# A graph network layer on one core: the last tile of every tenth gather group, fetched row by row through SyncE

## The chip, the cores and the metric

The kernel runs on one core of one Trainium2 chip. The metric is the device time of one execution in microseconds (us). Lower is better. The names of the engines are those of the profile: PE is the matrix engine (PEld its weight loads), DVE the vector engine, ACT the scalar engine, POOL GpSimd and SP SyncE. A name with a q, such as SPq, is that engine's sequencer, the part that waits, loads registers and issues DMAs.

## The reference

One message-passing layer over a graph with 12,500 nodes and 412,500 edges, the edges sorted by receiver:

```python
h = jnp.maximum(_layernorm(x, axis=-1), 0.0)
msg_in = jnp.concatenate([h[src], h[dst], edge_attr_32], axis=-1)       # 64 + 64 + 32
messages = swish(msg_in @ W1 + b1) @ W2 + b2
att = softmax(swish(msg_in @ Wa1 + ba1) @ Wa2 + ba2, axis=0)            # over all edges
aggregated = segment_sum(messages * att, dst, num_segments=12500)
upd_in = jnp.concatenate([h, aggregated], axis=-1)
out = x + swish(upd_in @ Wu1 + bu1) @ Wu2 + bu2
```

## The kernel before

**Tables.** Because `msg_in @ W` splits into a sender's, a receiver's and an edge's part, the kernel first computes two tables in device memory, one row of 128 floats (512 B) for each node: `ts_d` for the sender's part and `tr_d` for the receiver's part, each with the attention branch in columns 0 to 63 and the message branch in 64 to 127. They are written by lines 237 (SP) and 252 (ACT).

**Groups.** The edges are then worked off in one pass (`one_pass`), in groups of K = 8 tiles of P = 128 edges. There are T = 3224 tiles and NG = 403 groups. For each group g:

- `load(g)`, lines 366 to 401. POOL issues eight gathers (line 373). Each is one indirect DMA that fetches, for 128 edges, the row of `ts_d` that the edge's `src` names, into one of the eight slices of `gs`, a tile of 128 x 8 x 128 floats. The pool `gather` (line 170) holds eight such tiles. SP fetches the edges' features (`eo`, line 382) and receivers (`db`, line 385) for NQ = 4 groups at a time, and for every group two windows of `tr_d` rows into `wins` (line 392), whose place comes from a register; three `wins` buffers take turns. The registers are loaded four at a time (`registers`, line 360, a TENSOR_LOAD). DVE builds the one-hot matrix (line 396), and PE forms the receivers' and edges' part in PSUM (`pe`, line 400).
- `begin(g)`, lines 403 to 406. DVE adds `pe` and `gs` into `gs` (line 405); ACT takes the tanh (line 406).
- `end(g)`, lines 408 to 431. DVE forms messages and attention logits (lines 416 to 427).
- `by_node`, `out_of`, `project` and `put`, some five groups later. DVE weighs one-hot windows (line 468), PE sums the messages by node (lines 474 and 485), DVE adds them into `sums` (lines 495 to 499).

**Order.** The loop of lines 535 to 585 runs `begin(g)`, `load(g + 2)` and `end(g)` in turn, so PE's part of a group stands two groups ahead of the addition that needs it. Most DVE, PE and ACT instructions are pinned to program order; DMAs are not, and a scheduler places them. Each engine works its own queue in order. In the built program SP's DMAs carry eight semaphores in turn, and each DMA waits until the DMA that last used its semaphore, eight places back in the queue, has landed; POOL's gathers have eight of their own. SP's `wins` DMA for group g also waits until PE has read the same buffer for group g - 3.

**Beside it and behind it.** From group 16 on, once every four groups until the 98 blocks of nodes are done, `node_rest` and `node_bias` send five or six more DMAs through SP (lines 270, 279, 288, 290). Behind the pass, lines 588 to 630 compute the nodes' output. `general` is another path, taken only when the receivers spread too far; it is not taken here.

Of the kernel before, what the change touches and what calls it, by code (L numbers as in the profile page):

```python
# [42 lines left out]
F32 = mybir.dt.float32  # L43
I32 = mybir.dt.int32
AF = mybir.ActivationFunctionType
ALU = mybir.AluOpType
AX = mybir.AxisListType
ENG = mybir.EngineType
# [3 lines left out]
P = 128  # L52
# [3 lines left out]
C = 2 * U  # L56
S1 = U + 1
K = 8
# [7 lines left out]
B = 4  # L66
NQ = 4
TABLES = 4
EPS = 1e-5
NEG = -3.0e38  # L70
BIG = 3.0e38
WHY = "a receiver's number; windows past the last node are padded"


@with_exitstack
def gnn_kernel(ctx: ExitStack, tc: tile.TileContext, n_edges, x, src, dst, dst_row, first, edge,
               W1, b1, W2, b2, Wa1, ba1, Wa2, ba2, Wu1, bu1, Wu2, bu2, out):
    nc = tc.nc
    NB = x.shape[0] // P
    T = src.shape[1]  # L80
    NG = T // K
    NP = NB * P
# [6 lines left out]
    ts_d = dram.tile([NP, C], F32, name="ts_d")  # L89
# [13 lines left out]
    for r in range(2):  # L103
        for h, eng in ((0, nc.sync), (1, nc.scalar)):
            rows = slice(h * D, (h + 1) * D)
# [67 lines left out]
    with tc.tile_pool(name="node1", bufs=1) as node1, \  # L173
# [31 lines left out]
        for c in range(0, NB, CB):  # L205
# [9 lines left out]
            nc.vector.tensor_reduce(rstd, sq, AX.X, ALU.add)  # L215
            nc.vector.tensor_scalar(rstd, rstd, 1.0 / D, EPS, op0=ALU.mult, op1=ALU.add)
            nc.scalar.activation(rstd, rstd, AF.Sqrt)
# [5 lines left out]
            for b in range(0, CB, 8):  # L223
                n = min(8, CB - b)
# [16 lines left out]
        for c in range(0, NB, CB):  # L241
            tr = node.tile([P, CB, C], F32, name="tr")
            for b in range(0, CB, 4):
                n = min(4, CB - b)
                pn = node_ps.tile([P, 4, C], F32, name="pn", bufs=3)
                for i in range(0, n, 2):
# [5 lines left out]
            nc.scalar.dma_start(tr_d[:NP, :].rearrange("(p b) f -> p b f", b=NB)[:, c:c + CB, :], tr)  # L252

    one_pass(tc, n_edges, locals())
    again = nc.values_load(wrong[0:1, 0:1], min_val=0, max_val=1,
                           skip_runtime_bounds_check_because="it is the outcome of a comparison")
# [36 lines left out]
def one_pass(tc, n_edges, v):  # L293
    nc = tc.nc
    NB, T, NG, NP, CB = (v[k] for k in ("NB", "T", "NG", "NP", "CB"))
# [3 lines left out]
    ts_d, tr_d, bq_d, edge, dst_row = (v[k] for k in ("ts_d", "tr_d", "bq_d", "edge", "dst_row"))  # L299
# [8 lines left out]
    pin = tc.keep_in_program_order  # L308

    with ExitStack() as ctx:  # L310
# [22 lines left out]
        for w in wins:  # L333
            nc.vector.memset(w, 0.0)
            for r in range(2):
                rows = slice(WR + r * DE, WR + (r + 1) * DE)
                nc.vector.tensor_copy(w[rows, :, r, :], we[rows, None, :].to_broadcast([DE, 2, C]))
        with tc.tile_pool(name="work2", bufs=2) as work2, \
                tc.tile_pool(name="small", bufs=3) as small, \
                tc.tile_pool(name="pre_ps", bufs=AHEAD + 1, space=PSUM) as pre_ps, \  # L340
                tc.tile_pool(name="one_ps", bufs=1, space=PSUM) as one_ps:
            pes, gss, lgs, ps_, psums, sps, pps, ees, mts = ({} for _ in range(9))


            w2t_ps = one_ps.tile([P, 4, P], F32, name="mt")[:U, 0, :S1]
# [4 lines left out]
            nc.tensor.matmul(w2u_ps, w2t, wu1a, start=True, stop=True)  # L350
            nc.vector.tensor_copy(w2u, w2u_ps)
            at_sp, at_dve = {}, {}


            tr_w = bass.AP(tensor=tr_d.tensor, offset=tr_d.offset,
# [2 lines left out]
            def registers(g, engine, at):  # L358
                n = min(NQ, NG - g)
                _, regs = nc.values_load_multi_w_load_instructions(  # L360
                    base_sb[0:1, g:g + n], engines=[engine], min_val=0, max_val=NP - 1,
                    skip_runtime_bounds_check_because=WHY)
                for i in range(n):
                    at[g + i] = regs[i]

            def load(g):

                t = g * K
                if g % NQ == 0:
                    registers(g, ENG.SP, at_sp)  # L370
                gs = gss[g] = gather.tile([P, K, C], F32, name="gs")
                for j in range(K):
                    nc.gpsimd.indirect_dma_start(  # L373
                        out=gs[:, j, :], out_offset=None, in_=ts_d[:, :],
                        in_offset=bass.IndirectOffsetOnAxis(ap=src_sb[:, t + j:t + j + 1], axis=0))
                if g % NQ == 0:
                    n = min(NQ, NG - g) * E2
                    eo = work2.tile([P, NQ, E2], F32, name="eo")
                    db = work2.tile([WR, NQ, E2], I32, name="db")
                    for i in range(g, min(g + NQ, NG)):  # L380
                        ees[i] = eo[:, i - g, :], db[:, i - g, :]
                    nc.sync.dma_start(eo.rearrange("p g e -> p (g e)")[WR:, :n],
                                      edge[:, g * E2:g * E2 + n])
                    for r in range(2):
                        nc.sync.dma_start(
                            db.rearrange("p g e -> p (g e)")[r * R:(r + 1) * R, :n],
                            bass.AP(tensor=dst_row.tensor, offset=dst_row[r:r + 1, g * E2:].offset,
                                    ap=[[0, R], [1, n]]))
                eo, db = ees.pop(g)
                win = wins[g % WINS]  # L390
                for r in range(2):
                    nc.sync.dma_start(win[r * R:(r + 1) * R, :, r, :],
                                      tr_w[bass.ds(at_sp[g], R), :, :])
                for h in range(2):
                    e = slice(h * E2 // 2, (h + 1) * E2 // 2)
                    pin(nc.vector.tensor_scalar(eo[:WR, e], db[:, e], bj[:, g, h:h + 1], None,  # L396
                                                op0=ALU.is_equal))
                pe = pes[g] = pre_ps.tile([P, K, C], F32, name="pe")
                for q in range(H):
                    pin(nc.tensor.matmul(pe[:, 2 * q:2 * q + 2, :], eo[:, q * P:(q + 1) * P],  # L400
                                         win[:, q // 2, :, :], start=True, stop=True))

            def begin(g):

                pin(nc.vector.tensor_tensor(gss[g], pes[g], gss[g], ALU.add))  # L405
                pin(nc.scalar.activation(pes[g], gss[g], AF.Tanh))  # L406

            def end(g):
# [123 lines left out]
            for g in range(AHEAD):  # L532
                load(g)
            done = 0
            for g in range(NG):
# [3 lines left out]
                if more and g == NG - 1:  # L539
                    next(more)  # L540
                begin(g)
                if more and g < NG - 1:
                    next(more)
# [6 lines left out]
                if g + AHEAD < NG:  # L550
                    load(g + AHEAD)
# [36 lines left out]
        with tc.tile_pool(name="upd1", bufs=1) as upd1, \  # L588
# [14 lines left out]
            for c in range(0, NB, 2 * H):  # L603
                n = min(H, (NB - c) // 2)
# [32 lines left out]
def general(tc, n_edges, v, dst):  # L637
# [7 lines left out]
    with ExitStack() as ctx:  # L645
        keep = ctx.enter_context(tc.tile_pool(name="keep_g", bufs=1))
        act_d = dram.tile([P, T, S1], F32, name="act_d")
        sum_d = [dram.tile([NP + P, S1], F32, name=f"sum_d{r}") for r in range(TABLES)]
        before = keep.tile([P, P], F32, name="before")
# [15 lines left out]
        rows = (NP + P) // P  # L665
        for r in range(TABLES):
            flat = sum_d[r].rearrange("(p b) f -> p (b f)", p=P)
# [63 lines left out]
        with tc.tile_pool(name="sums_g", bufs=2) as work, \  # L731
                tc.tile_pool(name="sums_g_ps", bufs=2, space=PSUM) as sums_ps:
            for g in range(0, T, G):
# [3 lines left out]
                for k in range(0, ng, K):  # L737
# [26 lines left out]
                    for j in range(K):  # L764
                        nc.gpsimd.indirect_dma_start(
                            out=sum_d[(t + j) % TABLES][:, :],
                            out_offset=bass.IndirectOffsetOnAxis(ap=to[:, j:j + 1], axis=0),
# [6 lines left out]
        with tc.tile_pool(name="upd_g", bufs=2) as work, \  # L774
                tc.tile_pool(name="upd_g_ps", bufs=2, space=PSUM) as upd_ps:
            for c in range(0, NB, CB):
                part = work.tile([P, TABLES, CB, S1], F32, name="part")
                for r in range(TABLES):
                    nc.sync.dma_start(part[:, r], sum_v[r][:, c:c + CB, :])
                for r in range(1, TABLES):  # L780
                    nc.vector.tensor_tensor(part[:, 0], part[:, 0], part[:, r], ALU.add)
# [71 lines left out]
```

## Time and profile before

| | |
|---|---|
| median of 3 runs | 4180.05 us (4179.7 to 4185.37) |
| the profiled execution's own time | 4179.44 us |
| its span, first to last instruction | 4177.7 us |
| mean granted clock of PE | 0.635 of full speed |
| first and last gather (line 373) start | 75.3 and 4103.8 us |
| busy: POOL, DVE, PE, ACT | 3048.7, 2879.0, 2250.2, 600.1 us |

The span is counted from the first instruction of the profiled execution to its last; its own time is 1.7 us more. "Busy" is the time in which an engine worked, so POOL is busy for 73% of the span. An engine's wait, and the register and DMA-issuing instructions of a sequencer, are not counted as busy; they are found in the views by line and in the timeline. In the lists by group a line reads: source line, engine, operation, output and inputs, count, then busy time, mean time of one, and the idle time before it with what ended it.

### The profile page before, as it was taken

To read this page: it belongs to the slowest core of one execution; us is meant where nothing else is said; L and a number is where in the kernel's file an instruction comes from. 1 tells how busy PE (TensorE), PEld (TensorE's weight loads), DVE (VectorE), ACT (ScalarE), POOL (GpSimd) and SP (SyncE) were. 2 spreads that over 40 slices of the span, in tenths; PEclk is the share of its full clock that TensorE was granted. 3 is DMA by queue.
4 is the path that set the end of the run, shared out by engine and by line. 5 is a ranking of instruction groups with operands and counts; after the bars stand their busy time and mean duration, and the time that the engine had idled before them with its cause. 6 is when DMAs were issued, how large, how long until landed. Compare 5 with 4: busy or idle time off the path is not lost.

```text
span 4177.7 us, 43813 instructions
## 1 busy us (share of the span) xinstructions
PE 2250.2 (54%) x10980; PEld 1686.0 (40%) x10980; DVE 2879.0 (69%) x7713; ACT 600.1 (14%) x1229; POOL 3048.7 (73%) x3236
## 2 busy tenths in 40 slices
PE   5644556445555555555555555555555555555555
PEld 4433344333334433444334443343444334434344
DVE  5766767666767766766666666676676666766668
ACT  3211111111111111111111111111111111111112
POOL 2777777777777777777777777777777777777772
PEclk9566666666666666656666566566565665666665
DMA  6433334333333333333333333333323333333323
GB/s 246 112 86 101 101 95 102 96 100 103 95 95 91 83 88 89 81 89 83 87 89 80 89 86 84 90 80 90 90 80 90 82 88 90 80 90 82 87 77 110
DMA packets 232283, 392.22 MB, mean 94 GB/s; under 512 B 99797, under 2 KB 158294, under 8 KB 218838
## 3 DMA queue, kind: packets, MB, share of 16 engines
q0 software_dynamic: 103168, 211.49, 19.0%
q1 hardware_dynamic: 125808, 167.82, 15.3%
q10 hardware_dynamic: 3046, 10.02, 0.6%
q8 instruction: 91, 1.49, 0.2%
q14 instruction: 170, 1.39, 0.1%
HBM read 363.29 MB, written 25.72 MB: 93 GB/s over the span
## 4 chain that ended last, share of the span: by engine, by line


## 5 line engine op out<-in xcount | busy, mean ns | idle before, releaser
L373 POOL DMA_INDIRECT gs<-ts_d,src_sb x3224 | 3047.1, 945 | 1055.2 <-issue 884.1
L400 PE MATMUL pe<-wins,eo 128*128 128x256 f32 x3224 | 1405.3, 612 | 1183.2 <-issue 1132.6
L400 PEld LDWEIGHTS pe<-wins,eo 128*128 128x128 f32 x3224 | 959.6, 312 | 1460.3 <-issue 1198.1
L405 DVE TENSOR_TENSOR gs<-pe,gs 128x1024 f32<-128x1024 f32 x403 | 492.0, 1221 | 1115.7 <-DMA gs<-ts_d,src_sb 1108.2
L406 ACT ACTIVATE pe<-gs 128x1024 f32<-128x1024 f32 x403 | 415.6, 1031 | 2777.4 <-DVE gs L405 2315.9
L468 DVE TENSOR_SCALAR wt<-iota_w,dloc,p 128x40 f32<-128x40 f32 x3224 | 726.1, 317 | 0.1
L474 PE MATMUL sp<-wt,acts 128*65 128x40 f32 x6448 | 586.0, 261 | 0.9 <-DVE wt L468 0.9
L474 PEld LDWEIGHTS sp<-wt,acts 128*65 128x65 f32 x6448 | 535.3, 173 | 27.0 <-DVE wt L468 1.0
L444 PE MATMUL mt<-ident,mx 128*128 128x128 f32 x103 | 48.4, 470 | 515.0 <-DVE sums L498 508.8
L416 DVE SCALAR_TENSOR_TENSOR acts<-pe,gs 128x512 f32<-128x512 f32 x403 | 272.0, 675 | 27.6 <-ACT pe L406 27.6
L424 DVE TENSOR_TENSOR pe<-pe,wa 128x512 f32<-128x512 f32 x403 | 281.6, 699 | 12.8
L422 DVE SCALAR_TENSOR_TENSOR pe<-pe,gs 128x512 f32<-128x512 f32 x403 | 280.6, 696 | 11.5 <-ACT pe L406 0.2
L427 DVE TENSOR_REDUCE lg<-pe 128x8 f32<-128x512 f32 x403 | 276.9, 687 | 10.4
L396 DVE TENSOR_SCALAR eo<-db,bj 64x256 f32<-64x256 int32 x806 | 274.1, 378 | 7.6
L485 PEld LDWEIGHTS mt<-ss,w2u 65*64 65x64 f32 x806 | 99.8, 175 | 396.4 <-issue 383.4
L485 PE MATMUL mt<-ss,w2u 65*64 65x40 f32 x806 | 150.8, 281 | 162.9 <-DVE gm L451 150.9
L444 PEld LDWEIGHTS mt<-ident,mx 128*128 128x128 f32 x103 | 18.6, 180 | 528.2 <-DVE sums L498 521.1
L455 ACT ACTIVATE scale<-fall 128x1 f32<-128x1 f32 x103 | 20.9, 203 | 514.2 <-DVE fall L454 514.2
L499 DVE COPY sums<-nmax 64x40 f32 x403 | 79.6, 198 | 9.1 <-issue 0.3
L480 ACT COPY ss<-sp 65x40 f32<-65x40 f32 x403 | 73.4, 182 | 25.5 <-PE sp L474 25.3
L498 DVE TENSOR_TENSOR sums<-sums,mt 64x40 f32 x300 | 53.5, 178 | 2.9 <-PE mt L485 1.6
L275 ACT COPY bu<-mt 64x512 f32<-64x512 f32 x24 | 25.8, 1076 | 150.1 <-PE mt L272 144.4
(96 smaller groups left out, 596.7 us busy)
## 6 DMA issues: line engine op xcount, KB each, us to landing
gs<-ts_d,src_sb POOLq DMA_INDIRECT x3224
eo<-in_edge_dram SPq DMA_DIRECT2D x100, 512.0 KB
db<-in_dst_row_dram SPq DMA_DIRECT2D x200, 256.0 KB
wins<-tr_d SPq DMA_DIRECT2D x806, 32.0 KB
ts_d<-ts SPq DMA_DIRECT2D x7, 896.0 KB
tr_d<-tr ACTq DMA_DIRECT2D x7, 896.0 KB
xc<-in_x_dram SPq DMA_DIRECT2D x7, 448.0 KB
hT_d<-hT ACTq DMA_DIRECT2D x1, 3136.0 KB
```

Source lines behind the costliest of these rows:

```text
L373: nc.gpsimd.indirect_dma_start(out=gs[:, j, :], out_offset=None, in_=ts_d[:, :], in_offset=bass.IndirectOffsetOnAxis(ap=src_sb[:, t + j:t ...
L396: pin(nc.vector.tensor_scalar(eo[:WR, e], db[:, e], bj[:, g, h:h + 1], None, op0=ALU.is_equal))
L400: pin(nc.tensor.matmul(pe[:, 2 * q:2 * q + 2, :], eo[:, q * P:(q + 1) * P], win[:, q // 2, :, :], start=True, stop=True))
L405: pin(nc.vector.tensor_tensor(gss[g], pes[g], gss[g], ALU.add))
L406: pin(nc.scalar.activation(pes[g], gss[g], AF.Tanh))
L416: pin(nc.vector.scalar_tensor_tensor(acts[g % ACTS][:, :, 0:U], th[:, :, U:C], 1.0, gs[:, :, U:C], op0=ALU.add, op1=ALU.mult))
L422: pin(nc.vector.scalar_tensor_tensor(att, th[:, :, 0:U], 1.0, gs[:, :, 0:U], op0=ALU.add, op1=ALU.mult))
L424: pin(nc.vector.tensor_tensor(att, att, wa2[:, None, :].to_broadcast([P, K, U]), ALU.mult))
L427: pin(nc.vector.tensor_reduce(lgs[s][:, k:k + K], att, AX.X, ALU.add))
L468: pin(nc.vector.tensor_scalar(wt[:, j, :], iota_w[:, j // H, :], dloc[:, g * K + j:g * K + j + 1], p[:, k + j:k + j + 1], op0=ALU.is_equal ...
L474: pin(nc.tensor.matmul(sp, acts[g % ACTS][:, j, :], wt[:, j, :], start=j == 0, stop=j == K - 1))
L485: pin(nc.tensor.matmul(pp, w2u, sps.pop(g), start=True, stop=True))
```

## The change

For groups 10, 20, ..., 390 (39 of them) the eighth gather is left out. The 128 rows that it fetched come instead into a tile of their own, `one_gs`, over the ten groups before: in each `load(g)`, behind the `wins` DMAs, SP loads 13 of the 128 row numbers from `one_src` into registers with one TENSOR_LOAD (11 in the last of the ten groups) and issues one DMA of 512 B for each. The row numbers come into SBUF with one DMA of 512 B from a new input, `src_row`, the same numbers laid out in one row. In `begin(g)` of such a group the addition of 128 x 1024 becomes one of 128 x 896 and one of 128 x 128, the second reading `one_gs`. `work2` holds two buffers of `one_gs`.

```diff
+EVERY = 10
+ROWS = 13
+LOADS = 13
...
-            pes, gss, lgs, ps_, psums, sps, pps, ees, mts = ({} for _ in range(9))
+            pes, gss, lgs, ps_, psums, sps, pps, ees, mts, alone = ({} for _ in range(10))
...
+            rows_at, rows_to = {}, {}
+
+            def rows(g):
+                if g % EVERY == 0:
+                    t = (g + EVERY) * K + K - 1
+                    rows_to.clear()
+                    if g + EVERY < NG - 4:
+                        rows_to[g + EVERY] = one = work2.tile([P, C], F32, name="one_gs")
+                        alone[g + EVERY] = one
+                        rows_at[0] = small.tile([1, P], I32, name="one_src", bufs=2)
+                        nc.sync.dma_start(rows_at[0], v["src_row"][:, t * P:(t + 1) * P])
+                for to in rows_to.values():
+                    i = g % EVERY * ROWS
+                    for a in range(i, min(i + ROWS, P), LOADS):
+                        n = min(LOADS, P - a)
+                        _, regs = nc.values_load_multi_w_load_instructions(
+                            rows_at[0][0:1, a:a + n], engines=[ENG.SP], min_val=0, max_val=NP - 1,
+                            skip_runtime_bounds_check_because=WHY)
+                        for k in range(n):
+                            nc.sync.dma_start(to[a + k:a + k + 1, :], ts_d[bass.ds(regs[k], 1), :])
...
-                for j in range(K):
+                for j in range(K - (g in alone)):
                     nc.gpsimd.indirect_dma_start(
...
                     nc.sync.dma_start(win[r * R:(r + 1) * R, :, r, :],
                                       tr_w[bass.ds(at_sp[g], R), :, :])
+                rows(g)
...
-                pin(nc.vector.tensor_tensor(gss[g], pes[g], gss[g], ALU.add))
+                n = K - (g in alone)
+                pin(nc.vector.tensor_tensor(gss[g][:, :n, :], pes[g][:, :n, :], gss[g][:, :n, :], ALU.add))
+                if n < K:
+                    pin(nc.vector.tensor_tensor(gss[g][:, n, :], pes[g][:, n, :], alone.pop(g), ALU.add))
...
+        "src_row": padded(src, t * P)[None],
```

More of the change, by code (lines that the diff above doesn't have):

```diff
@@ L75, in gnn_kernel @@
 @with_exitstack
-def gnn_kernel(ctx: ExitStack, tc: tile.TileContext, n_edges, x, src, dst, dst_row, first, edge,
+def gnn_kernel(ctx: ExitStack, tc: tile.TileContext, n_edges, x, src, src_row, dst, dst_row, first, edge,
                W1, b1, W2, b2, Wa1, ba1, Wa2, ba2, Wu1, bu1, Wu2, bu2, out):
```

## The prediction

> **What bounds the kernel now.** I read the page first (busy times and groups), then POOL's timeline at the start, the view of the gathers' line, the waits, and last SP's own queue, since that is where the new work goes.
>
> ```profile
> L373 POOL DMA_INDIRECT gs<-ts_d,src_sb x3224 | 3047.1, 945 | 1055.2 <-issue 884.1
> L405 DVE TENSOR_TENSOR gs<-pe,gs 128x1024 f32<-128x1024 f32 x403 | 492.0, 1221 | 1115.7 <-DMA gs<-ts_d,src_sb 1108.2
> ```
>
> ```profile
> 75.35 1.10 POOL L373 DMA_INDIRECT gs<-ts_d,src_sb  x1 [72.95 <-DMA tr_d<-tr]
> 76.76 0.94 POOL L373 DMA_INDIRECT gs<-ts_d,src_sb  x1 [0.30 <-issue]
> 78.00 0.95 POOL L373 DMA_INDIRECT gs<-ts_d,src_sb  x1 [0.30 <-issue]
> ```
>
> ```profile
> L373 POOL DMA_INDIRECT gs<-ts_d,src_sb x3224: 940/944/1193, 75.3 to 4103.8; - x190
> ```
>
> POOL looks only 73% busy, but 0.30 us stands ahead of nearly every gather and nothing is waited for in it ("issue"): it belongs to the gather. From the first start (75.35) to the end of the last (4103.8 + 0.94) are 4029.4 us; over 3224 gathers that is **1.250 us each**, without a hole. Of the rest, 75 us lie before the first gather and 73 us behind the last. DVE, the next busiest, waits 1108.2 us for gathered rows, 2.75 us per group, so it has room. POOL's queue of gathers sets the end.
>
> SP's queue holds the rest of the evidence:
>
> ```profile
> SPq L392 <- PE pe L400: 1931.4, 275, 22.6
> ```
>
> ```profile
> PE pe L400 <- DMA wins<-tr_d: 14.9, 1, 14.9
> ```
>
> ```profile
> L392 SPq FUSED_REGOPS  x806: 37/37/51, 99.5 to 4062.5; - x162
> L392 SPq MOVE wins<-tr_d x806: 29/29/128, 99.6 to 4062.7; - x162
> L392 SPq DMA_DIRECT2D wins<-tr_d x806: 316/317/790, 99.7 to 4062.7; - x162
> ```
>
> ```profile
> 2022.76 0.82 SPq L392 DMA_DIRECT2D wins<-tr_d  x2
> ```
>
> SP waits 1931 us for PE to free `wins`, while PE waited for `wins` once only: SP runs up to three groups ahead, about 30 us.
>
> **What goes.** 39 gathers (groups 10 to 390) leave POOL's queue: 39 x 1.250 = **-48.7 us**. What is late next? DVE gets such a group after 8.75 us instead of 10.0; 10.0 less its 2.75 us of waiting is 7.25 us of work, so it still waits. Over ten groups POOL takes 79 x 1.250 = 98.7 us, **9.87 us per group**.
>
> **What DVE gains as work.** In 39 groups one addition becomes two. A 64x40 addition takes 0.18 us in the trace, which I take as the price of one more instruction. It also waits on up to eight semaphores of SP's DMAs; a sequencer's semaphore wait is a row of 17 ns with gaps of some 45 ns, so up to 0.5 us. Together 0.7 us, in 2.75 us of waiting: nothing at the end. Without that cover it would be 39 x 0.7 = 27 us.
>
> **What SP gains.** This decides. Two `wins` DMAs take 0.82 us from the first one's start to the second one's end, so start to start is 0.82 - 0.317 = 0.503 us: the DMA's own 0.317 and 0.186 for FUSED_REGOPS, MOVE and gaps. A row's DMA, from a register too, has the same sequence. Its own issue is unknown for one row; the nearest rows are three one-row DMAs of ACT's queue in the prologue:
>
> ```profile
> L137 ACTq DMA_DIRECT2D w2b<-in_b_dram x1: 251/251/251, 16.3 to 16.3; - x1
> L121 ACTq DMA_DIRECT2D base_sb<-in_first_dram x1: 291/291/291, 7.9 to 7.9; - x1
> L110 ACTq DMA_DIRECT2D w_bu<-in_bu_dram x1: 681/681/681, 1.4 to 1.4; - x1
> ```
>
> The bounds are 0.251 and 0.681. I take 0.29: that one stood close behind another DMA, as the rows will; 0.681 is from the program's first two microseconds, where most DMAs took 0.4 to 0.7. A row then costs 0.476 us of SP (0.437 to 0.867), and 12.8 rows per group 6.1 us (5.6 to 11.1).
>
> The TENSOR_LOAD of 13 registers:
>
> ```profile
> L360 SPq TENSOR_LOAD <-base_sb x101: 293/298/676, 98.9 to 4035.1; - x101
> L255 SPq TENSOR_LOAD <-wrong x1: 279/279/279, 4172.1 to 4172.1; - x1
> ```
>
> Four registers take 298 ns and one takes 279, so 6 ns each: 13 take 0.35, with a gap 0.40 us per group. The lower bound is 0.3; the upper one is 13/4 x 0.298 = 0.97, if each register cost in proportion.
>
> Here the Trainium skill speaks against the change. "Runtime: NRT & Kernel Launch", section Instruction fetch mechanics, says that a load into sequencer registers takes about 200 ns for each register, even in bulk. By it, 13 registers would be 2.6 us per group, SP would need 2.2 us more than in the sum below and pass POOL's pace, and by the working of rival 1 the kernel would end some 350 us or more behind the forecast. It speaks of loads from device memory; `base_sb` lies in SBUF, and its 6 ns per register decide.
>
> Per ten groups SP also issues `one_src` and waits for it. `hb<-in_x_dram`, issued at 115.80, released DVE's line 289 at 118.16, 2.0 us after its issue ended, so 2.5 us, 0.25 per group.
>
> Landing: each DMA waits for the one eight places back. Eight rows of 0.476 are 3.8 us, more than those 2.0, so rows alone do not stall. Behind `eo` and two `db` (1 MB, at the best slice's 246 GB/s 4.2 us) a row can wait 4.2 + 2.0 - 3.8 = 2.4 us, once in four groups: up to 0.6 per group.
>
> SP's old work per group: two `wins` 1.0, a quarter of `eo` (0.48), two `db` (0.41) and a TENSOR_LOAD (0.30) with gaps 0.45, semaphore waits 0.1: 1.6 us. While the node work runs (about groups 18 to 116), a quarter of lines 288, 290, 279 and two of 270 (0.40, 0.39, 0.49, 2 x 0.61, gaps) adds 0.7.
>
> The sum per group: 1.6 + 6.1 + 0.4 + 0.25 + (0 to 0.6) = **8.35 to 8.95 us**, and 9.05 to 9.65 with node work, against POOL's 9.87. SP keeps up, narrowly. The `wins` of a group may come up to 30 us late before PE asks for them, and POOL has eight `gs` buffers, so a short excess is absorbed.
>
> Who waits behind a waiting row? The next group's `wins`, then PE's line 400, then DVE's line 405. SP's last rows for group 10m stand behind `wins` of 10m - 1, which PE uses in iteration 10m - 3; the addition that needs them is three groups (30 us) later. The packets carry the same bytes as before; landings shift a little, but POOL waits for none that matters (53 us in 0.3 us pieces, all of them the usual gap).
>
> **Sum.** 4179.4 - 48.7 = 4130.7 for the profiled execution; it lies 0.6 us under the median, so about **4131 us** (-1.2%).
>
> **Rivals.**
> 1. *SP becomes the bound: slower.* In SP's queue, rows hold up `wins`, and PE starves. Load 389, the last with rows, must be done when iteration 388 begins, 75 + 389 x 9.87 + 3 = 3918 us by POOL's pace; SP reaches it at 97 + 390 W + 70 (node work). So it decides from W = 9.62 us, that is a row of (9.62 - 2.85)/12.8 = 0.53 us (0.58 without the stall behind `eo`), and the gain is used up at W = 9.74. Against it: `wins` itself, with 64 rows, takes 0.503. For it: with `db`'s median of 0.414 a row takes 0.60, W is 10.5, and the end comes at 4131 + 97 + 4095 + 70 - 3918 = 4475 us; with 0.681, W is 13.35 and the end 5590.
> 2. *SP falls behind in the node stage only.* At the dearer end (0.503 per row) W is 2.3 + 6.4 + 0.4 + 0.25 + 0.6 = 10.0 there, 0.1 over for 100 groups; with SP's waits for DVE's line 289 and ACT's line 275 (108 and 17 us in the waits) perhaps 60 us of lag, of which 30 of lead and some buffers are cover. Price up to 40 us: 4131 to 4171.
> 3. *The removed gather is not the one that counts:* DVE waits for the last row in each such group for what POOL saves, 1.25 us: 4180. Against it stand the three groups between them.
>
> **How the numbers follow.** The forecast 4131 has 0.72 (4127 to 4136; no more than 39 gathers can be gained), rival 2 has 0.09, rival 3 has 0.04, rival 1 has 0.15. The range, 4126 to 4172, leaves out rivals 1 and 3. A measurement here tells 0.2% (8 us) from no change. Faster: 0.72 + 0.09 = 0.81; within 0.2%: 0.04; slower: 0.15.
>
> **What would show it.** Right: 3185 gathers still 1.25 us apart; line 405 still released by the gathers' DMA; SP's DMA of a row near 0.29 us and start to start near 0.48; a TENSOR_LOAD of 13 near 0.35; SPq still waiting for PE at `wins`, perhaps a third of 1931 us. Wrong: POOL with idle time before gathers released by DVE; PE's line 400 released by `wins` often; rows over 0.53 us apart.

## The result and the profile after

The change made the kernel slower: 4213.40 us (4213.05 to 4216.91, 4 runs) against 4181.07 us (4179.7 to 4185.37, 4 runs), a ratio of 1.0079 with a 95% interval of 1.0065 to 1.0094. The profiled execution took 4216.91 us, with a span of 4215.1 us, 37.4 us more than before. In experiments 1 to 4 the profiled execution of each kernel run more than once was 1 to 8 us shorter than its others, so each ratio is to runs of the kernel before that were taken beside it, and profiled times are compared with profiled times.

In the changed kernel the gathers are line 397, the one-hot 421, PE's receiver part 425, the addition 431 (and 433 for `one_gs`), the row numbers 372, the rows 376, `wins` 416. The groups and the row of the gathers' line:

```profile
L397 POOL DMA_INDIRECT gs<-ts_d,src_sb x3185 | 3019.4, 948 | 1121.1 <-issue 949.9
L425 PE MATMUL pe<-wins,eo 128*128 128x256 f32 x3224 | 1436.9, 623 | 1639.9 <-DMA wins<-tr_d 633.4
L421 DVE TENSOR_SCALAR eo<-db,bj 64x256 f32<-64x256 int32 x806 | 260.5, 361 | 862.0 <-DMA db<-in_dst_row_dram 821.4
L431 DVE TENSOR_TENSOR gs<-pe,gs 128x1024 f32<-128x1024 f32 (+1 forms) x403 | 485.8, 1206 | 80.6 <-PE pe L425 28.5
```

```profile
L397 POOL DMA_INDIRECT gs<-ts_d,src_sb x3185: 938/944/1194, 75.4 to 4141.9; - x200
L397 POOLq EVENT_SEMAPHORE  x398: 42/43/13137, 74.3 to 4125.6; - x199
```

The 39 gathers are gone, yet the last one starts 38.1 us later (4141.9 against 4103.8). DVE's addition hardly waits for gathered rows any more (1108.2 us before, 27.0 now); DVE and PE wait at the start of a group instead, for `db` (821 us) and `wins` (633 us), both of which come through SP. PE's many waits for `wins` are one of the signs that the prediction named as "wrong"; rows over 0.53 us apart, another, did not come. SP's own waits, in its queue, say the same from the other side:

```profile
SPq L372 <- DMA one_src<-in_src_row_dram: 86.1, 37, 4.8
...
SPq L416 <- PE pe L425: 43.9, 15, 9.1
...
SPq L376 <- DMA db<-in_dst_row_dram: 28.6, 36, 1.3
```

The wait for PE at `wins`, SP's spare time, fell from 1931.4 us to 43.9. SP hardly waits for anything: it is always working, and late. Its rows and the gaps of up to 0.2 us between them, taken together, fill some 95% of the time (before, 22% in the node stage and 15% behind it).

Where POOL loses time is seen in its timeline, about 600 us into the run (start, duration, instruction, idle time before it):

```profile
609.79 0.94 POOL L397 DMA_INDIRECT gs<-ts_d,src_sb  x1 [0.31 <-issue]
611.81 0.61 DVE L421 TENSOR_SCALAR eo<-db,bj 64x256 f32<-64x256 int32 x2 [7.16 <-DMA db<-in_dst_row_dram]
...
612.66 3.75 PE L425 MATMUL pe<-wins,eo 128*128 128x256 f32 x8 [7.18 <-DMA one_gs<-ts_d]
...
614.74 0.70 DVE L450 SCALAR_TENSOR_TENSOR pe<-pe,gs 128x512 f32<-128x512 f32 x1
615.47 0.70 DVE L452 TENSOR_TENSOR pe<-pe,wa 128x512 f32<-128x512 f32 x1
616.19 0.94 POOL L397 DMA_INDIRECT gs<-ts_d,src_sb  x1 [5.46 <-issue]
```

POOL stands still for 5.46 us and goes on after DVE's line 450, the last reader of an old `gs`, has ended. The view calls the gap "issue", which reads as if POOL waited for nothing. It waited for a buffer, in its sequencer: that is the EVENT_SEMAPHORE row above, whose longest took 13.1 us. The one before this gap ended at 615.47, 0.04 us after line 450, and so, within 0.05 us, did every one of the 92 that took over 0.5 us. (PE's line 425 does not read `one_gs`, which the view names there; it reads the one-hot that DVE's line 421 finished at 612.42, 0.24 us before.)

By stages (time, then busy time and count of PE, PEld, DVE, ACT and POOL, clock, DMA share, GB/s), before and then after:

```profile
600.00:1450.00 850.00, 457.33 (x2294) 333.30 (x2295) 597.34 (x1630) 124.65 (x254) 642.76 (x681) 0.65 0.37 95
1450.00:4000.00 2550.00, 1373.36 (x6698) 1032.59 (x6697) 1745.20 (x4722) 324.43 (x702) 1928.14 (x2041) 0.62 0.33 86
```

```profile
600.00:1450.00 850.00, 459.80 (x2104) 331.76 (x2102) 550.86 (x1503) 117.31 (x233) 586.51 (x619) 0.61 0.36 91
1450.00:4000.00 2550.00, 1392.64 (x6857) 1052.81 (x6858) 1788.71 (x4863) 339.20 (x721) 1928.18 (x2034) 0.63 0.35 87
```

All the loss lies in the node stage: there POOL did 619 instructions in place of 681. Behind it POOL runs at its old rate (2034 against 2041), with fewer gathers to a group, so the other engines get through more groups.

The account of POOL's queue closes. 39 x 1.250 = -48.7 us. Of the gaps between gathers 25 were longer than 0.5 us (the 22 over 1.3 us all lie between 600 and 1480 us); above the usual 0.305 they add +77.1. A gather took 948.0 ns on average and not 945.1: 3185 x 2.9 ns = +9.1. The sum is +37.5; the last gather came 38.1 us later and the span grew by 37.4.

DVE's steps show SP's pace. Line 431 started for group 40 at 533 us, for group 120 at 1404, for 140 at 1600 and for 380 at 3943: **10.9 us per group** in the node stage and **9.76** behind it, against POOL's 9.87. When DVE began group 20 POOL was 4.1 groups ahead of it, at group 60 it was 6.9, with eight buffers in all (2.2 at both places before): the buffers were used up by 600 us, and from there SP's excess of 1 us per group came straight out of POOL's time.

And one instruction makes SP's excess, as experiments 1 and 5 will show. The rows of the new work, and SP's timeline in two stretches of the later stage:

```profile
L372 SPq TENSOR_LOAD <-one_src x390: 970/2832/3262, 101.0 to 4017.0; - x195
```

```profile
L376 SPq FUSED_REGOPS  x4992: 37/37/47, 102.0 to 4023.7; - x200
L376 SPq MOVE one_gs<-ts_d x4992: 29/29/42, 102.1 to 4023.8; - x200
L376 SPq DMA_DIRECT2D one_gs<-ts_d x4992: 224/228/308, 102.2 to 4023.8; - x200
```

```profile
2004.44 0.86 SPq L416 DMA_DIRECT2D wins<-tr_d  x2
2008.40 5.24 SPq L376 DMA_DIRECT2D one_gs<-ts_d  x13
```

A row's DMA costs less than was forecast: 0.228 us of its own, and 13 of them take 5.24 us, so (5.24 - 0.228)/12 = 0.42 us from start to start (0.476 forecast). But from the end of `wins` (2005.30) to the first row (2008.40) stand 3.1 us, and 2.86 of them are the TENSOR_LOAD of 13 numbers. On average it took 2.28 us, not 0.35. Even the old load of four numbers, 298 ns before, had grown:

```profile
L384 SPq TENSOR_LOAD <-base_sb x101: 313/496/682, 99.0 to 4072.4; - x101
```

The 390 loads are not alike. They go by where in `one_src` the 13 numbers begin:

| first number | begins at a multiple of | TENSOR_LOAD, us (usual values) |
|---|---|---|
| 0, 52, 104 | 4 words | 0.97 to 1.18 |
| 26, 78 | 2 words, not 4 | 2.68 or 2.86 |
| 13, 39, 65, 91 | 1 word | 2.86 |
| 117 (11 numbers) | 1 word | 2.46 |

### The profile page after: what moved, and what is told of

Its sections match the earlier page's. It is cut to its first block, busy times and chain, and to the rows that moved or that the text cites. A ratio compares the mean times of both kernels' runs of the same rounds, so it can differ in the third digit from the quotient of the medians.

```text
span 4215.1 us, 59401 instructions
## 1 busy us (share of the span) xinstructions
PE 2284.3 (54%) x10980; PEld 1713.3 (41%) x10980; DVE 2885.7 (68%) x7752; ACT 609.6 (14%) x1229; POOL 3020.9 (72%) x3197
## 4 chain that ended last, share of the span: by engine, by line
## 5 line engine op out<-in xcount | busy, mean ns | idle before, releaser
L425 PE MATMUL pe<-wins,eo 128*128 128x256 f32 x3224 | 1436.9, 623 | 1639.9 <-DMA wins<-tr_d 633.4
L425 PEld LDWEIGHTS pe<-wins,eo 128*128 128x128 f32 x3224 | 980.5, 319 | 1928.1 <-issue 1666.5
L421 DVE TENSOR_SCALAR eo<-db,bj 64x256 f32<-64x256 int32 x806 | 260.5, 361 | 862.0 <-DMA db<-in_dst_row_dram 821.4
L431 DVE TENSOR_TENSOR gs<-pe,gs 128x1024 f32<-128x1024 f32 (+1 forms) x403 | 485.8, 1206 | 80.6 <-PE pe L425 28.5
```

The costliest lines, as they stand in the source:

```text
L431: pin(nc.vector.tensor_tensor(gss[g][:, :n, :], pes[g][:, :n, :], gss[g][:, :n, :], ALU.add))
```

## The experiments

Two theories were open. **A**: SP became the bound by its own work, through the load of the registers, whose price hangs on the place of the first number. **B**: SP is held by the landings of the small DMAs, each of which waits for the one eight places back. A third possibility was that the work itself is hidden and the rows disturb the gathers in memory.

**1. `e1_aligned`: the same numbers, each group's 13 beginning at a multiple of 16 words.**

```diff
-rows_at[0] = small.tile([1, P], I32, name="one_src", bufs=2)
+rows_at[0] = small.tile([1, EVERY * 16], I32, name="one_src", bufs=2)
...
-rows_at[0][0:1, a:a + n]
+rows_at[0][0:1, i // ROWS * 16:i // ROWS * 16 + n]
...
-"src_row": padded(src, t * P)[None],
+"src_row": ...   # (t, 10, 16): 13 numbers, then 3 zeros
```

> The same rows, with the row numbers laid out so that each group's 13 begin on a multiple of 16 words; nothing else changes. Theory A (SP is the bound, by the load of 13 registers, which is slow where its first word is not on a multiple of four): the load falls from 2.29 us on average to 1.0 to 1.2 us in every group, SP needs 9.7 us per group in the node stage and 8.6 behind it against POOL's 9.87, POOL never stalls, and the time is 4131 us (4127 to 4140). Theory B (SP's queue is held up by landings, each DMA waiting for the one eight places back, or PE and DVE by later windows and receivers behind the rows): the load may shorten, but the queue waits instead, and the time stays over 4180 us.

Measured: 4142.89 us (4141.34 to 4143.33) against 4185.79 for the kernel before, measured beside it, a ratio of **0.9897** (0.9881 to 0.9914): the same rows, the same number of DMAs (`one_src` alone grows from 512 to 640 B), and the loss is a gain. The time lies 3 us over the range expected; the kernel before was itself some 5 us slower beside it (4185.79 against 4181.07). The load, POOL's line and the stages:

```profile
L372 SPq TENSOR_LOAD <-one_src x390: 971/1157/1655, 101.0 to 3903.8; - x195
```

```profile
L397 POOL DMA_INDIRECT gs<-ts_d,src_sb x3185: 940/947/1194, 75.6 to 4066.6; - x200
L397 POOLq EVENT_SEMAPHORE  x398: 42/43/43, 74.5 to 4050.3; - x199
```

```profile
600.00:1450.00 850.00, 476.98 (x2292) 349.59 (x2291) 598.25 (x1624) 124.44 (x251) 643.02 (x678) 0.64 0.42 98
1450.00:4000.00 2550.00, 1419.28 (x6820) 1065.32 (x6818) 1781.93 (x4825) 329.76 (x713) 1929.56 (x2035) 0.62 0.37 88
```

POOL's semaphore waits are all 43 ns, no gap is over 0.5 us, and the node stage has 678 POOL instructions again. DVE does fall behind there, to 4.9 groups at group 120 (10.15 us per group), and catches up later (1.2 at group 160): the eight buffers cover it. The line of additions shows who is late again:

```profile
L431 DVE TENSOR_TENSOR gs<-pe,gs 128x1024 f32<-128x1024 f32 (+1 forms) x403 | 487.4, 1210 | 750.2 <-DMA gs<-ts_d,src_sb 715.9
```

This version is faster than both kernels. B falls: as many small DMAs land as in the change, and by B the time would have stayed over 4180 us.

**2. `e2_no_rows`: the gathers go, and nothing comes in their place.** The eighth tile of the 39 groups lacks the sender's part.

```diff
+                if g % EVERY == 0 and 0 < g < NG - 4:
+                    alone[g] = None
...
-                rows(g)
...
-nc.vector.tensor_tensor(gss[g][:, n, :], pes[g][:, n, :], alone.pop(g), ALU.add)
+nc.vector.tensor_copy(gss[g][:, n, :], pes[g][:, n, :])
```

> The gather of the eighth tile is left out in the same 39 groups and nothing is fetched in its place, so the sender's part of those 39 tiles is left out; DVE still does two instructions there. Both theories: POOL saves 39 x 1.250 us and nothing takes its place, 4131 us (4129 to 4134). A third reading, that a gather less does not shorten POOL's queue by its whole slot, would give 4140 to 4180.

Measured: 4137.16 us (4130.27 to 4137.76), a ratio of 0.9884 (0.9867 to 0.99). The profiled execution took 4130.27 us, 48.2 less than before's beside it (4178.51). Its median is 2 us over the range expected.

```profile
L399 POOL DMA_INDIRECT gs<-ts_d,src_sb x3185 | 3010.4, 945 | 1043.2 <-issue 882.7
```

So the term of the removed gathers was right to 0.5 us, and it is all that leaving them out can gain. Experiment 1 is 5.7 us above it by the medians, 11.1 by the profiled executions. In the latter the gathers account for it: 948.4 ns in place of 945.2, times 3185, is 10.4 us. The rows are not shown to be the reason: in experiment 3, with as many rows in each of its 270 groups, a gather took 945.4 ns on average, and in experiment 4, with one row per group, 947.9.

**3. `e3_from_130`: rows for groups 130 to 390 only, so none while the node work runs.** The loads stay where they were, seven of ten at a dear place.

```diff
-                    if g + EVERY < NG - 4:
+                    if 120 <= g and g + EVERY < NG - 4:
...
+                        if g == 120:
+                            pin(nc.vector.memset(rows_at[0], 0))
```

> Rows only for groups 130, 140, ..., 390 (27 of them), fetched from load 120 on, behind the node stage; the loads of registers are as in the changed kernel. Theory A, with the stage where SP falls behind being the node stage: behind it SP needs 9.78 us per group against POOL's 9.87, POOL never stalls, 27 x 1.250 = 33.7 us are saved: 4147 us (4143 to 4153). The reading that the rows cost as much wherever they stand: 27/39 of the 32 us lost, some 4204 us.

Measured: 4154.33 us (4147.3 to 4154.94), a ratio of 0.9925 (0.9908 to 0.9941); profiled 4147.3 us. 27 gathers x 1.25 = 33.8 us under 4178.5 would be 4144.8. The median is 1 us over the range expected, and far from the 4204 of the other reading.

```profile
L374 SPq TENSOR_LOAD <-one_src x270: 972/2851/2878, 1276.7 to 3923.3; - x135
```

```profile
SPq L418 <- PE pe L427: 497.5, 95, 22.4
```

The loads are as dear as in the change (2.28 us on average), and POOL has no gap over 0.5 us: behind the node stage SP's pace fits within POOL's 9.87, with little to spare, and the whole loss is made in the node stage. (Part of SP's wait for PE is from the groups before the first rows.) The old load of four numbers shows a second effect here: 0.31 us in the groups before the first rows and 0.50 from there on, always from a multiple of four.

**4. `e4_probe`: the price of the load by itself.** The kernel before, with one more TENSOR_LOAD in each group, of 1, 2, 4, 8, 13 or 16 words, from 16 different places of `base_sb`, and one row's DMA (into a tile that DVE clears first).

```diff
+n, a = (1, 2, 4, 8, 13, 16)[g % 6], 64 + g // 6 % 16
+_, regs = nc.values_load_multi_w_load_instructions(base_sb[0:1, a:a + n], engines=[ENG.SP], ...)
...
+nc.sync.dma_start(dummy, ts_d[bass.ds(regs[n - 1], 1), :])
```

> The kernel before, with one more load of registers per group on SP, of 1, 2, 4, 8, 13 or 16 words from base_sb, its first word at each of 16 places in turn; the last of the registers is used for one row's DMA into a tile that nobody reads. No gather is left out. SP is idle three quarters of the time here. Theory A: 0.28 us for one word and 0.2 us for each further word where the first word is off a multiple of four (13 words 2.7 to 2.9 us, 16 words 3.3 to 3.5), and 0.2 us for each further four words on it (4 words 0.30, 8 words 0.5, 16 words 0.9 to 1.1, 13 words 1.0 to 1.2). Its rival: the load is long in the changed kernel since it waits for what stands ahead of it in a full queue; here all are 0.28 to 0.40 us. The time stays within 0.3% of before under both, since 3.9 us more per group find SP idle.

Measured: 4188.83 us, one run. All its loads, and by size and place:

```profile
L395 SPq TENSOR_LOAD <-base_sb x403: 274/977/4123, 100.4 to 4088.7; - x135
```

| words | first at a multiple of 4 | at 2 words past | at an odd word |
|---|---|---|---|
| 1 | 0.29 | 0.28 | 0.47 |
| 2 | 0.67 | 0.66 | 0.66 |
| 4 | 0.50 | 1.06 | 0.87 |
| 8 | 0.72 | 1.87 | 1.86 |
| 13 | 0.98 | 2.68 | 2.86 |
| 16 | 1.17 | 3.46 | 3.46 |

(us, the usual value; some loads were 0.19 or 0.26 us longer, and with what that goes was not found.) Off the multiple of four, a longer load costs 0.2 us more for every word (3.46 - 1.86 over 8 words). On it, four words more cost 0.22 us (1.17 - 0.72 over 8 words), and 13 words, three fours and one, 0.98. Most of the expected prices came, and the rival (0.28 to 0.40 us for all) is out; missed were one word at an odd place (0.47, not 0.28), two words (0.66 at every place) and the loads of four and eight on the multiple (0.2 us dearer). The place works in `base_sb` as it does in `one_src`, so it isn't the tile that is dear. The table is not a fixed price list: four words on the multiple took 0.30 us in the kernel before and 0.50 here, in the change and in experiment 3 behind its first rows; what raises them was not tested.

**5. `e5_one_word_off`: experiment 1 with each chunk one word further on,** so that all ten loads of a round are dear. Nothing else differs: same tile, same size, same DMAs.

```diff
-rows_at[0][0:1, i // ROWS * 16:i // ROWS * 16 + n]
+rows_at[0][0:1, i // ROWS * 16 + 1:i // ROWS * 16 + 1 + n]
...
-"src_row": ...   # (t, 10, 16): 13 numbers, then 3 zeros
+"src_row": ...   # (t, 10, 16): a zero, 13 numbers, then 2 zeros
```

> The aligned kernel with every group's 13 row numbers one word further on in the same tile, and nothing else. Theory A (the load of registers sets SP's pace): every load takes 2.86 us instead of 1.0 to 1.2, also 0.57 us more than the changed kernel's average of 2.29, so that SP needs 10.35 us per group behind the node stage and is the bound to the end: 4213 + 390 x 0.57 = 4435 us (4340 to 4440; the low end if SP's waits shrink by what the loads grow). Theory B (landings and queued windows, not the load): as the aligned kernel, 4131 to 4145 us.

Measured: 4359.33 us (4357.3 to 4361.82) against 4181.53, a ratio of **1.0427** (1.041 to 1.0445).

```profile
L372 SPq TENSOR_LOAD <-one_src x390: 2450/2854/3304, 100.4 to 4170.4; - x195
```

```profile
600.00:1450.00 850.00, 439.67 (x2026) 313.70 (x2025) 532.59 (x1449) 113.69 (x227) 567.87 (x600) 0.62 0.36 88
1450.00:4000.00 2550.00, 1339.49 (x6564) 1010.00 (x6565) 1711.26 (x4645) 326.82 (x689) 1870.59 (x1974) 0.63 0.34 84
```

The mean load is 2.79 us. One word of displacement costs some 220 us (ratios of 1.0427 and 0.9897). Now the later stage loses as well (1974 POOL instructions for 2035): DVE's line 431 goes at 11.2 us per group in the node stage and 10.2 behind it, over POOL's 9.87 in both, so the lag never shrinks (still 6.75 groups at group 380). The change itself lies between 1 and 5, as its three cheap loads in ten put it.

**6. `e6_singly`: each number loaded by a TENSOR_LOAD of its own.**

```diff
-LOADS = 13
+LOADS = 1
```

> The changed kernel with each row number loaded by a load of its own, one register at a time. Theory A: a load of one word takes 0.28 us at an even place and 0.47 at an odd one, with its gap 0.43 on average, 5.5 us per group in place of 2.34: 390 x 3.15 = 1230 us more, 5440 us (5250 to 5500). Theory B: no load is long, so the time is at most the changed kernel's 4213 us.

Measured: 6117.83 us, one run: the direction was right and the size missed (618 us over the range).

```profile
L372 SPq TENSOR_LOAD <-one_src x4992: 275/501/1056, 100.1 to 5939.1; - x200
```

A lone load among the rows took 0.505 us on average, not the 0.375 that is the mean of the table's 0.28 and 0.47. With it the sum comes near: a row with its load took 0.99 us from start to start, so (0.99 - 0.42) x 12.8 - 2.3 = 5.0 us more per group, for 390 groups 1950 us, and 4213 + 1950 is 6163. (DVE's line 431 goes at 15.6 us per group in the node stage and 14.7 behind it, 4.7 and 5.0 more than in the change.) Place makes no difference here, 0.50 us at odd and even numbers alike; why a load between rows is dearer than the same load of the probe was not tested.

**7. `e7_eighth`: experiment 1 with a gather left out in every eighth group and 16 rows in each,** 49 gathers in place of 39.

```diff
-EVERY = 10
-ROWS = 13
-LOADS = 13
+EVERY = 8
+ROWS = 16
+LOADS = 16
```

> The aligned kernel with the last tile of every eighth group fetched by rows, 16 rows per group and one aligned load of 16: 49 gathers less, POOL would end 61 us earlier, near 4120 us, if SP had room (theory B, where short aligned loads leave only landings). Theory A: SP's measured work in the aligned kernel, 8.85 us per group, grows by 3.2 rows of 0.41 and 0.2 for the longer load to 10.4 with 0 to 0.4 of waits, against POOL's 9.84: SP is the bound, 4500 us (4430 to 4600).

Measured: 4419.45 us, one run, 11 us under the range expected.

```profile
L397 POOL DMA_INDIRECT gs<-ts_d,src_sb x3175: 938/945/1197, 75.7 to 4307.9; - x199
L397 POOLq EVENT_SEMAPHORE  x398: 42/2772/14765, 74.6 to 4291.4; - x199
```

```profile
L372 SPq TENSOR_LOAD <-one_src x392: 973/1160/1839, 101.0 to 4238.3; - x196
```

The loads are cheap here, and SP is over the line all the same: three rows more are 3.2 x 0.42 = 1.3 us per group, DVE's line 431 goes at 10.17 us per group behind the node stage, and half of POOL's waits for a buffer are 2.8 us or longer (the usual one was 43 ns before). So the load by itself is not the bound; SP's sum is, and in the change the load carried it over.

## Why the prediction was wrong

The forecast was 4131 us and faster; it came to 4213.4 and slower.

- **The gathers, -48.7 us: right.** Experiment 2 gave -48.2 between the profiled executions.
- **The TENSOR_LOAD of 13 registers: the step that failed.** The prediction took 0.40 us per group, with 0.97 as its upper bound; it was 2.28 us and a gap. The 6 ns per register came from one pair of rows, 298 ns for four registers and 279 for one. The first was `base_sb[0:1, g:g + n]` with g a multiple of four, so always four words from a multiple of four; the second was a single word of another tile, `wrong`. The slope was drawn through two loads for which most of the change's first words (13, 26, 39, ...) were no case. The 298 ns did not even hold for their own line, which took 496 in the change. The upper bound, "in proportion", came from the same rows and so had the same blind spot: 0.97 us turned out to be the price of the cheapest load. The Trainium skill's "Runtime: NRT & Kernel Launch", section Instruction fetch mechanics, weighed there and set aside, states about 200 ns for each register. The 0.2 us per word measured off the multiple of four agrees with it; 13 words on the multiple, 0.98 us or 0.075 each, are far below.
- **The rows: mis-sized the other way,** 0.476 us forecast, 0.42 measured, 0.7 us less per group. It took back a third of the error.
- **The landings (0 to 0.6 us per group): small.** SP waited 28.6 us in all at the rows for `db`, 0.07 per group; the wait for `one_src` was 86 us in 37 rounds, within the 0.25 per group set for it.
- **SP's sum:** 8.35 to 8.95 us forecast, 9.05 to 9.65 with node work. Measured were paces of 9.76 and 10.9. Putting 2.33 for 0.40 and 0.42 for 0.476 into the prediction's own sum gives 9.6 to 10.2 and 10.3 to 10.9, which about holds both. With the landings as small as they were, the low ends are the ones to compare: the later stage fits (9.6 against 9.76), and the node work, put at 0.7, came to 1.1 us per group (10.9 - 9.76), a second term that was too small.
- **The rivals.** Rival 1 (SP becomes the bound) has the right engine and even the right pace: its formula, 97 + 390 W + 70 with the measured 9.76, and 1.1 us more for each of the 98 or so groups of the node stage in place of its 70, ends at 4011 us; SP's last row was issued at 4023.8. But it looked for the cause in a row over 0.53 us, and the rows stayed under. Rival 2 had the place (the node stage alone) and a mechanism that holds, lead and buffers used up and the rest paid; its 0.1 us per group was 1.0, and its price of up to 40 us was 77. The range ended 41 us too low because both rivals were priced by the row and neither by the load.
- **DVE's new work: hidden, as said.** Line 433 took 0.28 us (0.18 forecast), and rival 3 (DVE waits for the last row) is out: in experiment 1 the additions wait for the gathers again, and its time is within 11 us of experiment 2's.
- **"POOL waits for none that matters":** not quite. POOL waited for buffers, 77 us in all. A gather was also 3 ns longer on average in the change (948 against 945), 9 us over the pass; no term stood for that, and its cause is open.

## What to carry to other kernels

A duration taken from a row holds for what that row did: before a price per element is drawn from two rows, look at what else they share (here the place of the first word) and whether the new instruction shares it. When a change hands work to an engine that runs ahead, add up its pace stage by stage against the pace of the bound; an excess is paid first from lead and buffers, so the loss appears late, at another engine, and under a name like "issue". Row numbers that a sequencer loads in bulk should begin at a multiple of four words: in this kernel that padding is worth some 75 us (ratios of 1.0079 without and 0.9897 with it).

## What the runs showed of the hardware

- A TENSOR_LOAD of 8 to 16 words from SBUF on SP's queue took 0.2 us per word, unless its first word lay at a multiple of four words; then 13 words took 0.98 us in place of 2.86 (between rows mostly 1.16), and 16 took 1.17 in place of 3.46. One or two words took 0.28 to 0.67 us. The price also hangs on something else: the same line's load of four words took 0.30 us without the rows and 0.50 with them.
- SP issues a one-row DMA with its place in a register every 0.42 us, its own issue being 0.228 us, in 4992 of them and with landings that held it for 29 us in all.
- The gathers' mean length moved between 945 and 948 ns from run to run, but not with the rows: it was 945.4 in experiment 3 and 944.7 in experiment 6, which have them, and 947.9 in experiment 4, which has one per group. In experiment 1 the usual length was 947 in place of 944; in the change it was 944 and single ones were longer. What sets it is open.
